# Attention with top-1 experts: row sums sent by DMA to 128 partitions of 16, inverted at once, read back 32-fold from DRAM; weights in three tiles, projections spread evenly

## The chip, the core and the metric

The kernel runs on one core of a Trainium2 chip. The time is the device time of one execution in microseconds (us); the median of several runs is compared. A profile of one further execution shows what each engine did and when.

The engines are TensorE (PE in the profile, with its weight loads as PEld), VectorE (DVE), ScalarE (ACT), GpSimd (POOL) and SyncE (SP), which here only issues transfers. Each works through its own instructions in order. TensorE writes into PSUM, of which this kernel uses eight banks of 128 x 512 numbers as one tile called `array`.

## The reference

x has 4 batches of 2,048 tokens of width 512. It is normalized, and attention and an expert layer of the normalized x are added to x:

```python
xn = _layernorm(x, axis=-1)
x = x + attn(xn, w_qkv, w_out, b_out, mask_logits) + ffn(xn, w_gate, w_expert, b_expert)

# attn: 16 heads of 32
q, k, v = split(xn @ w_qkv)                  # to heads
q, k = filter(q), filter(k)                  # rfft, times a sigmoid mask, irfft
scores = einsum('bhqd,bhkd->bhqk', q, k) / sqrt(32)
out = einsum('bhqk,bhkd->bhqd', softmax(scores), v)
return out @ w_out + b_out

# ffn: each token goes to the best of 8 experts, the first 100 tokens of each expert are
# kept; a kept row is gate * (row @ w_expert + b_expert), all other rows are 0
```

All is float32. The filter is linear, so the kernel folds it into the query and key weights at its start.

## The kernel before

**Groups, blocks, steps.** The work runs over 16 head groups k (4 batches by 4 groups of 4 heads; b, c = divmod(k, 4)), in each over 4 query blocks n of 512 queries, in each over 16 key tiles j of 128 keys. One key tile of one block is a step here (a "half" in the code: two make a window). There are 16 x 4 x 16 = 1,024 steps, 64 to a group and 16 to a block.

In each step TensorE does, for its block, two times two score products (`scores`, tiles `q` and `steps_of_keys`) into banks 0 to 3, ScalarE takes their exponentials into a tile `even` or `odd`, and the value products (`products`) of the step before follow; VectorE adds those into `num`. The scores are shifted by the maximum of their row, which has to be known before a block starts. So a second stream of products (`keys`, `q`) runs 20 steps (40 pieces, `MAX_AHEAD`) ahead; VectorE reduces each to its maximum (`max_reduce`, tile `part`), in one instruction for two banks that lie side by side, or in two (`apart`). Four steps before a block opens, the maxima are turned by TensorE (`max_close`: `square`, `neg`), split into three bfloat16 rows by POOL (`max_split`: `rest`, `row`) and sent by SP to a tile `negm`; four products of `negm` open the block (`shift`). The maxima's products, value products, projections and all the rest share banks 4 to 7 in rotation (`bank`), so a product waits until the engine that reads the bank's old content is done.

**Row sums.** The exponentials' tiles of a block are added up in pairs by a DMA that adds in place (`even<-odd`, 1 MB, issued by POOL) and then by POOL's additions (`even<-even`). Five steps after a block's end TensorE adds over the keys (`fold`, product with ones), ScalarE copies the sums to `den`. Each sum stands there on 32 partitions. VectorE inverts `den` in eight pieces of 64 columns, one per step (`invert`); POOL multiplies `num` by it (`divide`, tile `ot`) before step 14, TensorE projects with `wo` (`result`), ScalarE copies to `y`, and POOL issues a DMA that adds `y` to the output in DRAM (`add`).

**Projections.** While group k runs, the queries, keys and values of group k + 1 are made in 48 pieces of 128 tokens (`query_key`, `value`). A planner (`spread`) puts a list of steps with costs and earliest times into the agenda of the 64 steps; `costs` holds what is there already. The pieces stand in an order written out by hand (`projections`); keys can't be written before the maxima of group k are past them (`SPENT`). The weights of a group lie in one tile `wg`, reloaded once all pieces are done, so the list ends three steps before the group's end.

**A new batch.** In the third group of a batch (k = 2, 6, 10) the next batch's x is loaded tile by tile (`load_tile`), measured by VectorE, given the bias `b_out` by POOL (`bias`) and written to the output as its first sums (`first_sums`). In the fourth group x is loaded again, normalized and turned by TensorE. In group 0 the first sums of batch 0 are made in this way too.

The agenda of a step runs after its products, and `max_close` stands before it. Every engine's instructions keep the program's order (`InOrder`). In the profile nearly all of them have line 84, that helper's, so they are told apart by tile names.

Of the kernel before, what the change touches and what calls it, by code (L numbers as in the profile page):

```python
# [39 lines left out]
PART = 64  # L40
# [63 lines left out]
def attention_and_top1_experts(ctx: ExitStack, tc: tile.TileContext, a: dict, out: bass.AP):  # L104
# [90 lines left out]
    def filter_steps(c):  # L195

        held = {}

        def turned(s):
            if s == 0:  # L200
                held["wt"] = probs(c % 2 == 1)
            pt = bank()
            for r in range(NR):
                on.tensor.transpose(
                    pt[:, r * P : (r + 1) * P], raw[s, r // 2][:, r % 2, c * P : (c + 1) * P], ident
                )
            on.vector.tensor_copy(held["wt"][:, s, 0, :], pt)

        def filtered(s):
            pw = bank()  # L210
            wt = held["wt"][:, s]
            for r in range(NR):
                at = slice(r * P, (r + 1) * P)
                on.tensor.matmul(pw[:, at], lhsT=wt[:, 0, at], rhs=filt, start=True, stop=True)
            done = pw.rearrange("p (r n) -> p r n", r=NR)
            if c == 0:
                on.scalar.copy(wg[0][:, :, s, :], done)
# [12 lines left out]
    def token_stage(b):  # L230
# [20 lines left out]
        def bias(i):  # L251
            row = held[i // TQ][:, i % TQ, :]
            on.gpsimd.tensor_tensor(row, row, b_out, ALU.add)

        def first_sums(i):

            n, t = divmod(i, TQ)
            on.sync.dma_start(out=o[b, n, :, t : t + 1, :], in_=held[n][:, t : t + 1, :])
# [149 lines left out]
        return load, measure, scale, normalize, turn, route, bias, first_sums, load_tile  # L408
# [5 lines left out]
    def load_qkv_weights(k):  # L414
        wg[k] = weights.tile([P, NR, 3, P], F32, name="wg", bufs=1)
        on.sync.dma_start(out=wg[k], in_=wd[k % NG])
# [12 lines left out]
    def query_key(k, n, s, first, last):  # L429

        here, cols = slice(first * P, last * P), slice(n * QB + first * P, n * QB + last * P)
        pq = bank()[:, here]
        for r in range(NR):
            columns(pq, wg[k][:, r, s, :], xnT[:, r, cols], start=(r == 0), stop=(r == NR - 1))
# [17 lines left out]
    def value(k, n, first, last):  # L452
        if n == 0 and first == 0:
            vs[k] = qkv.tile([P, NT, P], F32, tag="v", name="v")
        pv = bank()
        for t in range(first, last):
            i = n * TQ + t
            for r in range(NR):
                columns(
                    pv[:, t * P : (t + 1) * P],  # L460
                    xnT[:, r, i * P : (i + 1) * P],
                    wg[k][:, r, 2, :],
                    start=(r == 0),
                    stop=(r == NR - 1),
                )
# [3 lines left out]
    def projections(k, tiles=1):  # L469

        if k == 0:
            order = [(query_key, 0, 1), (query_key, 0, 0)]
            order += [(query_key, n, 1) for n in range(1, NQ)] + [(query_key, 1, 0)]
            order += [(value, n) for n in range(NQ)] + [(query_key, n, 0) for n in range(2, NQ)]
        else:
            late = [(value, n) for n in range(2, NQ)] + [(query_key, 1, 0)]
            order = [(query_key, 0, 0)] + [(value, n) for n in range(2)] + (late if k not in CROWDED else [])
            order += [(query_key, n, 1) for n in range(NQ)] + (late[::-1] if k in CROWDED else [])
            order += [(query_key, n, 0) for n in range(2, NQ)]
# [72 lines left out]
    def expert_steps():  # L552


        def begin():
            w_exp = chunk("w_exp")
            on.sync.dma_start(out=w_exp, in_=a["L0_ffn_w_expert"].rearrange("(r p) n -> p r n", p=P))
            b_exp = b_out
# [130 lines left out]
    def close_steps(k, n):  # L689
# [25 lines left out]
        if (k, n) == (B * NG - 1, NQ - 2):  # L715
            steps = [(7, 1, fold)] + [(8 + i // 2, 0, invert, i) for i in range(QB // PART)]
            first = 12
# [22 lines left out]
    load, measure, scale, normalize, turn, first_route, first_bias, first_sums, load_tile = token_stage(0)  # L740
# [5 lines left out]
    wg[0] = weights.tile([P, NR, 3, P], F32, name="wg", bufs=1)  # L746
    nc.sync.dma_start(out=wg[0][:, :, 2, :], in_=w_qkv[:, :, 2 * DM : 2 * DM + P])
# [12 lines left out]
    nc.sync.dma_start(out=wd[0], in_=wg[0])  # L760
# [51 lines left out]
    for i, item in enumerate(stream[:MAX_AHEAD]):  # L812
# [6 lines left out]
        max_reduce(item, half)  # L819
# [83 lines left out]
    def keys_from(k):  # L903

        return (9 if k in CROWDED else 6) * TQ

    def plan(k):
# [4 lines left out]
        def after_keys_are_spent(steps, start):  # L912

            first = len(steps) - keys_from(k + 1)
            for i in range(NT):
                cost, _, step = steps[first + i]
                steps[first + i] = cost, start + SPENT + i // TQ * TQ, step

        if k == 0:
            for i in range(NT):  # L920
                half = 2 + i + 5 * (i // TQ)
                at(half, load_tile, i)
                at(half + 4, first_bias, i)
                at(half + 6, first_sums, i)
# [3 lines left out]
        last = start + GH - 4  # L928
        steps = []
        if k == 0:  # L930
            done = spread([(1, 0, step) for step in first_projections], 15)
            at(done[-1] + 1, load_qkv_weights, 1)
            plan_route(20, lambda i: first_route[i]())
            ready = done[-1] + 3
        if c == NG - 2 and b + 1 < B:

            at(start + 20, begin_stage, b + 1)
            for i in range(NT):
                half = start + 20 + i + 5 * (i // TQ)
                at(half, in_stage, 8, i)  # L940
                at(half + 3, in_stage, 1, i)
                at(half + 4, in_stage, 6, i)
                at(half + 6, in_stage, 7, i)
            for n in range(NQ):
                at(start + 30 + (TQ + 5) * n, in_stage, 2, n * TQ, (n + 1) * TQ)
            for i in range(2 * TQ):
                at(start + GH - 6 + i, in_stage, 8, i)
        pieces = projections(k + 1)
        if c == NG - 1:
# [3 lines left out]
            order += pieces[4:8] + [("turn", i) for i in range(12, NT)] + pieces[8:]  # L953
            steps, first = [], start + 1
            for step in order:
                if isinstance(step, tuple):
                    i = step[1]
                    steps.append((1, start + late[i] if i in late else 0, lambda i=i: in_stage(4, i)))
                else:
                    steps.append((1, 0, step))  # L960
            steps[0] = (1, first, steps[0][2])
            after_keys_are_spent(steps, start)
# [4 lines left out]
            for i in range(2 * TQ, NT):  # L967
                at(turned[i // TQ * TQ - TQ - 1] + 1 + i % TQ, in_stage, 8, i)
            plan_route(turned[NT - 1] + 2, follow_route)
        else:  # L970
            steps = [(1, ready if k == 0 else start, step) for step in pieces]
            after_keys_are_spent(steps, start)
            done = spread(steps, last)
        assert done[-4] >= start + 3 * HB and done[-8] >= start + 2 * HB
        for i in range(NT):
            here = done[len(done) - keys_from(k + 1) + i] - start - i // TQ * TQ
            assert SPENT <= here < SPENT + 3 * TQ
# [17 lines left out]
    for block in range(1, B * NG * NQ):  # L995

        costs[block * HB - 4] += 0.5
# [15 lines left out]
    for k in range(B * NG):  # L1013
        for n in range(NQ):
            num = work.tile([P, QB], F32, tag="num", name="num")
            tiles = {}
            for w in range(NW):
# [9 lines left out]
                for j in (even, odd):  # L1027
# [5 lines left out]
                    for u in range(2):  # L1033
# [7 lines left out]
                        if mate:  # L1041
                            max_reduce(mate, mh)
# [63 lines left out]
```

## Time and profile before

| | |
|---|---|
| median of 3 runs | 4,277.05 us (4,273.49 to 4,280.85) |
| profiled execution | 4,282.12 us, span 4,280.0 us, granted TensorE clock 0.993 |
| TensorE busy | 4,194.3 us, 52,270 instructions |
| VectorE busy | 3,411.0 us; of it maxima `part` 2,497.1, `num` 650.3, reciprocals 274.3 |
| POOL busy | 3,037.6 us; of it additions `even` 2,121.5 |
| ScalarE busy | 2,525.3 us |
| DMA, software queue (POOL) | 605.83 MB, 72.1% of 16 engines' span |
| DMA, hardware queue (SP) | 76.10 MB, 5.7% |

The page gives busy time, the chain of work that ended last, and groups of instructions with their mean duration. The timeline gives single instructions: start, duration, engine, operation, tile written <- tiles read, shapes, count; brackets hold the idle time before it and what ended it. A float32 product is two instructions.

### The profile page before, as it was taken

To read this page: it belongs to the slowest core of one execution; us is meant where nothing else is said; L and a number is where in the kernel's file an instruction comes from. 1 tells how busy PE (TensorE), PEld (TensorE's weight loads), DVE (VectorE), ACT (ScalarE), POOL (GpSimd) and SP (SyncE) were. 2 spreads that over 40 slices of the span, in tenths; PEclk is the share of its full clock that TensorE was granted. 3 is DMA by queue.
4 is the path that set the end of the run, shared out by engine and by line. 5 is a ranking of instruction groups with operands and counts; after the bars stand their busy time and mean duration, and the time that the engine had idled before them with its cause. 6 is when DMAs were issued, how large, how long until landed. Compare 5 with 4: busy or idle time off the path is not lost.

```text
span 4280.0 us, 120579 instructions
## 1 busy us (share of the span) xinstructions
PE 4194.3 (98%) x52270; PEld 1854.3 (43%) x52270; DVE 3411.0 (80%) x5102; ACT 2525.3 (59%) x3475; POOL 3037.6 (71%) x2110
## 2 busy tenths in 40 slices
PE   8999999999999999999999999999999999999998
PEld 4444444434444444443444444443444444444432
DVE  6767888877788888887778888887778887788885
ACT  2556655666566556557556666555755565556665
POOL 1678777876776767777677766778668776676773
PEclk9999999999999999999999999999999999999999
DMA  4767778887687778888677787888877886778788
GB/s 109 179 149 152 153 160 173 191 201 151 137 159 153 156 152 165 182 195 186 132 158 151 158 159 146 170 188 194 170 140 152 175 164 131 148 162 161 154 168 167
DMA packets 163452, 690.16 MB, mean 161 GB/s; under 512 B 27414, under 2 KB 32696, under 8 KB 97640
## 3 DMA queue, kind: packets, MB, share of 16 engines
q0 software_dynamic: 110432, 605.83, 72.1%
q1 hardware_dynamic: 51312, 76.10, 5.7%
q8 instruction: 409, 6.70, 0.6%
q14 instruction: 123, 1.01, 0.1%
q10 hardware_dynamic: 1176, 0.52, 0.1%
HBM read 59.27 MB, written 88.96 MB: 35 GB/s over the span
## 4 chain that ended last, share of the span: by engine, by line
PE 89%; DVE 6%; DMA 2%; POOL 2%; issue 1%; ACT 0%; ACTq 0%; POOLq 0%; DVEq 0%
PE array L84 89%; DVE part L84 4%; DMA even<-odd 2%; POOL even L84 1%; DVE num L84 0%; DVE stats L84 0%; DMA negm<-row 0%; DVE factor L84 0%; POOL xs L84 0%; DMA odd<-in_L_attn_w_qkv_dram 0%; DVE mv L84 0%; POOL row L84 0%; POOL rstd L84 0%; DVE even L84 0%; POOL rest L84 0%
## 5 line engine op out<-in xcount | busy, mean ns | idle before, releaser
L84 DVE TENSOR_REDUCE part<-array 128x1 f32<-128x512 f32 (+1 forms) x3336 | 2497.1, 805 | 761.6 <-PE array L84 758.3
L84 POOL TENSOR_TENSOR even<-even 128x1024 f32<-128x1024 f32 x876 | 2121.5, 2524 | 425.9 <-DMA even<-odd 417.8
L84 PE MATMUL array<-keys,q 32*128 32x512 f32 x8192 | 2089.7, 615 | 10.9 <-DVE part L84 5.5
L84 PE MATMUL array<-q,steps_of_keys 32*128 32x512 f32 x8192 | 2022.7, 618 | 3.3 <-ACT odd L84 1.7
L84 ACT ACTIVATE even<-array 128x1024 f32<-128x1024 f32 x1024 | 993.5, 1021 | 491.3 <-PE array L84 455.6
L84 ACT ACTIVATE odd<-array 128x1024 f32<-128x1024 f32 x1024 | 993.3, 1021 | 458.8 <-PE array L84 378.5
L84 PEld LDWEIGHTS array<-keys,q 32*128 32x128 f32 x8192 | 784.3, 185 | 591.3 <-DVE part L84 365.3
L84 PEld LDWEIGHTS array<-q,steps_of_keys 32*128 32x128 f32 x8192 | 707.2, 184 | 267.3 <-issue 233.1
L84 POOL DMA_DIRECT2D even<-odd x510 | 463.4, 909 | 402.2 <-ACT odd L84 321.4
L84 DVE TENSOR_TENSOR num<-num,array 128x512 f32<-128x512 f32 x960 | 650.3, 677 | 26.3 <-PE array L84 17.2
L84 PE MATMUL array<-odd,v 128*32 128x512 f32 x4096 | 549.4, 608 | 2.4 <-DVE part L84 2.4
L84 PE MATMUL array<-even,v 128*32 128x512 f32 x4096 | 547.4, 606 | 2.9 <-DVE part L84 2.9
L84 PEld LDWEIGHTS array<-xnT,wg 128*32 128x32 f32 x15808 | 439.0, 110 | 256.2 <-DVE part L84 176.2
L84 PE MATMUL array<-xnT,wg 128*32 128x128 f32 (+1 forms) x15808 | 522.0, 277 | 11.4 <-DVE part L84 10.6
L84 PEld LDWEIGHTS array<-wg,xnT 128*32 128x32 f32 x8192 | 227.9, 110 | 129.2 <-DVE part L84 94.4
L84 DVE RECIPROCAL factor<-den 128x64 f32<-128x64 f32 x504 | 274.3, 545 | 0.0
L84 PE MATMUL array<-wo,ot 128*32 128x512 f32 x2048 | 267.8, 596 | 4.0 <-POOL ot L84 4.0
L84 PE MATMUL array<-wg,xnT 128*32 128x128 f32 x8192 | 263.5, 273 | 4.4 <-DVE part L84 4.4
L84 PEld LDWEIGHTS array<-odd,v 128*32 128x32 f32 x4096 | 81.0, 108 | 394.1 <-DVE part L84 384.9
L84 PEld LDWEIGHTS array<-even,v 128*32 128x32 f32 x4096 | 80.8, 108 | 393.8 <-DVE part L84 382.7
L84 POOL DMA_DIRECT2D out_dram<-y x63 | 83.7, 1329 | 212.4 <-ACT y L84 190.9
L84 ACT COPY y<-array 128x512 f32<-128x512 f32 x252 | 147.5, 586 | 139.8 <-PE array L84 139.4
(129 smaller groups left out, 1490.5 us busy)
## 6 DMA issues: line engine op xcount, KB each, us to landing
even<-odd POOLq DMA_DIRECT2D x510, 1024.0 KB, 8.2
out_dram<-y POOLq DMA_DIRECT2D x63, 1024.0 KB, 10.1
xs<-in_L_attn_x_dram SPq DMA_DIRECT2D x112, 256.0 KB
out_dram<-xs SPq DMA_DIRECT2D x64, 256.0 KB
wg<-wd SPq DMA_DIRECT2D x15, 768.0 KB
wo<-in_L_attn_w_out_dram SPq DMA_DIRECT2D x16, 256.0 KB
negm<-row SPq DMA_DIRECT2D x192, 4.0 KB
xs<-in_L_attn_x_dram SPq DMA_DIRECT2D x2, 1024.0 KB
```

Source lines behind the costliest of these rows:

```text
L84: done = act(*args, **kwargs)
```

## The change

The eight reciprocals of a block give way to one. SP sends one copy of each row sum (`den`, every 32nd partition, 4 x 512) to 128 partitions of 16 columns (`apart`); VectorE inverts these 128 x 16 (`invert`); SP writes them to DRAM (`lay_down`) and reads them back so that each head's row of 512 lands on its 32 partitions (`to_rows`, four transfers). These steps stand one, two, three and four steps after the fold.

The weights of queries, keys and values lie in three tiles, each reloaded after its own last piece. The order of the pieces is new: values first, then queries and keys, and the list may end on the group's last step. Turns are planned at a cost of 0.5 instead of 1, the block's fixed cost at 0.25 instead of 0.5.

The first sums are x itself, copied from DRAM to DRAM 1 MB at a time; the bias is added by VectorE where the result of the first group of a batch leaves PSUM. `b_exp` has a tile of its own. Loads and statistics of a new batch stand at other steps. `max_close` follows the agenda of its step. Maxima of a step's first pair are reduced apart, those of its second pair apart only where the step has no planned cost; in the 40 pieces ahead of the first step none is kept apart on purpose.

```diff
+APART = HG * QB // P
-        def bias(i):
-            on.gpsimd.tensor_tensor(row, row, b_out, ALU.add)
-        def first_sums(i):
-            on.sync.dma_start(out=o[b, n, :, t : t + 1, :], in_=held[n][:, t : t + 1, :])
+        def first_sums(n):
+            on.sync.dma_start(out=o[b, n], in_=x[b, n])
...
-    def load_qkv_weights(k):
-        wg[k] = weights.tile([P, NR, 3, P], F32, name="wg", bufs=1)
-        on.sync.dma_start(out=wg[k], in_=wd[k % NG])
+    def load_qkv_weights(k, s):
+        wg[k, s] = weights.tile([P, NR, P], F32, name=f"w{s}", bufs=1)
+        on.sync.dma_start(out=wg[k, s], in_=wd[k % NG][:, :, s, :])
...
+            first = 2 if k in CROWDED else 3 if k % NG == 0 else 4
+            queries, vals = ([(f, n, *s) for n in range(NQ)] for f, *s in ((query_key, 0), (value,)))
+            news = [(query_key, n, 1) for n in range(NQ)]
+            if first == 4:
+                order = vals + queries[:2] + news + queries[2:]
+            else:
+                order = vals[:first] + queries[:1] + news[:3]
+                order += vals[first : first + 1] + news[3:] + vals[first + 1 :] + queries[1:]
...
-    def max_reduce(item, half):
+    def max_reduce(item, half, apart=True):
-        whole = joined(*half) if u == 0 else joined(*half, apart=True)
-        for heads, products_of in whole:
+        for heads, products_of in joined(*half, apart):
...
-        def invert(i):
-            at = slice(i * PART, (i + 1) * PART)
-            on.vector.reciprocal(held["factor"][:, at], held["den"][:, at])
+        def apart():
+            on.sync.dma_start(out=held["factor"][:, 0:APART], in_=held["den"][0::DH, :])
+        def invert():
+            at = held["factor"][:, 0:APART]
+            on.vector.reciprocal(at, at)
+        def lay_down():
+            held["all"] = scratch.tile([P, APART], F32, name="inverses")
+            on.sync.dma_start(out=held["all"], in_=held["factor"][:, 0:APART])
+        def to_rows():
+            for h in range(HG):
+                row = held["all"][DH * h : DH * (h + 1), :].rearrange("r c -> (r c)")
+                on.sync.dma_start(out=held["factor"][DH * h : DH * (h + 1), :], in_=row.partition_broadcast(DH))
...
-            on.scalar.copy(held["y"][:, t, :], project(k, held["ot"], t))
+            if k % NG == 0:
+                on.vector.tensor_tensor(held["y"][:, t, :], project(k, held["ot"], t), b_out, ALU.add)
+            else:
+                on.scalar.copy(held["y"][:, t, :], project(k, held["ot"], t))
...
-            steps = [(5, 1, fold)] + [(6 + i, 0, invert, i) for i in range(QB // PART)]
-            first = 17
+            begin, first = 5, 17
+        steps = [(begin, 1, fold)]
+        steps += [(begin + 1 + i, 0, step) for i, step in enumerate((apart, invert, lay_down, to_rows))]
...
-        last = start + GH - 4
+        last = start + GH - 1
...
-            at(done[-1] + 1, load_qkv_weights, k + 2)
+            for s in range(3):
+                at(places[s][-1] + 1, load_qkv_weights, k + 2, s)
...
-        costs[block * HB - 4] += 0.5
+        costs[block * HB - 4] += 0.25
...
-                            max_reduce(mate, mh)
+                            max_reduce(mate, mh, u == 0 or not costs[2 * window + (j == odd)])
...
+                    for step in agenda[2 * window + (j == odd)]:
+                        step()
                     if j == even and window in full:
                         splits[window + 1] = full.pop(window)
                         max_close(*splits[window + 1])
-                    for step in agenda[2 * window + (j == odd)]:
-                        step()
```

More of the change, by code (lines that the diff above doesn't have):

```diff
@@ L39 @@
 SCALE = 1.0 / math.sqrt(DH)
-PART = 64
+APART = HG * QB // P
 WIN = 2
@@ L216, in filtered @@
             if c == 0:
-                on.scalar.copy(wg[0][:, :, s, :], done)
+                on.scalar.copy(wg[0, s], done)
             else:
@@ L249, in measure @@
             on.vector.bn_aggr(mv[:, i, :], stats[:, i, :])
-        def bias(i):
-            row = held[i // TQ][:, i % TQ, :]
-            on.gpsimd.tensor_tensor(row, row, b_out, ALU.add)
-        def first_sums(i):
-            n, t = divmod(i, TQ)
-            on.sync.dma_start(out=o[b, n, :, t : t + 1, :], in_=held[n][:, t : t + 1, :])
+        def first_sums(n):
+            on.sync.dma_start(out=o[b, n], in_=x[b, n])
         def scale(first=0, last=NT, shift_on=None):
@@ L407, in token_stage @@
         route += [lambda i=i: enter(i) for i in range(NT)]
-        return load, measure, scale, normalize, turn, route, bias, first_sums, load_tile
+        return load, measure, scale, normalize, turn, route, first_sums, load_tile
     qs, vs = {}, {}
     wo = {}
-    def load_qkv_weights(k):
-        wg[k] = weights.tile([P, NR, 3, P], F32, name="wg", bufs=1)
-        on.sync.dma_start(out=wg[k], in_=wd[k % NG])
+    def load_qkv_weights(k, s):
+        wg[k, s] = weights.tile([P, NR, P], F32, name=f"w{s}", bufs=1)
+        on.sync.dma_start(out=wg[k, s], in_=wd[k % NG][:, :, s, :])
     def load_out_weights(k):
@@ L433, in query_key @@
         for r in range(NR):
-            columns(pq, wg[k][:, r, s, :], xnT[:, r, cols], start=(r == 0), stop=(r == NR - 1))
+            columns(pq, wg[k, s][:, r, :], xnT[:, r, cols], start=(r == 0), stop=(r == NR - 1))
         if s == 0:
@@ L461, in value @@
                     xnT[:, r, i * P : (i + 1) * P],
-                    wg[k][:, r, 2, :],
+                    wg[k, 2][:, r, :],
                     start=(r == 0),
@@ L467, in value, with projections @@
         on.scalar.copy(vs[k][:, n * TQ + first : n * TQ + last, :], done)
-    def projections(k, tiles=1):
+    def projections(k, tiles=1, kinds=None):
+        kinds = [] if kinds is None else kinds
         if k == 0:
@@ L475, in projections @@
         else:
[L476 to L479, printed above, removed]
+            first = 2 if k in CROWDED else 3 if k % NG == 0 else 4
[6 more added lines that the diff above has]
+                order += vals[first : first + 1] + news[3:] + vals[first + 1 :] + queries[1:]
+        kinds.extend((2 if f is value else at[1]) for f, *at in order for t in range(0, TQ, tiles))
         return [
@@ L557, in begin @@
             on.sync.dma_start(out=w_exp, in_=a["L0_ffn_w_expert"].rearrange("(r p) n -> p r n", p=P))
-            b_exp = b_out
+            b_exp = work.tile([P, DM], F32, tag="b_exp", name="b_exp", bufs=1)
             on.sync.dma_start(out=b_exp, in_=a["L0_ffn_b_expert"].partition_broadcast(P))
@@ L715, in close_steps @@
         if (k, n) == (B * NG - 1, NQ - 2):
-            steps = [(7, 1, fold)] + [(8 + i // 2, 0, invert, i) for i in range(QB // PART)]
-            first = 12
-        else:
-            steps = [(5, 1, fold)] + [(6 + i, 0, invert, i) for i in range(QB // PART)]
-            first = 17
+            begin, first = 7, 12
+        else:
+            begin, first = 5, 17
+        steps = [(begin, 1, fold)]
+        steps += [(begin + 1 + i, 0, step) for i, step in enumerate((apart, invert, lay_down, to_rows))]
         steps += [(first + t, 1, result, t) for t in range(TQ)]
@@ L737, in close_last @@
                 on.sync.dma_start(out=o[b, n, :, t - 1 : t + 1, :], in_=y[:, t - 1 : t + 1, :])
-    load, measure, scale, normalize, turn, first_route, first_bias, first_sums, load_tile = token_stage(0)
+    load, measure, scale, normalize, turn, first_route, first_sums, _ = token_stage(0)
     load(0)
@@ L745, in attention_and_top1_experts @@
     load(3, probs(False).rearrange("p u h q -> p (u h) q"))
-    wg[0] = weights.tile([P, NR, 3, P], F32, name="wg", bufs=1)
-    nc.sync.dma_start(out=wg[0][:, :, 2, :], in_=w_qkv[:, :, 2 * DM : 2 * DM + P])
+    for s in range(3):
+        wg[0, s] = weights.tile([P, NR, P], F32, name=f"w{s}", bufs=1)
+    nc.sync.dma_start(out=wg[0, 2], in_=w_qkv[:, :, 2 * DM : 2 * DM + P])
     for c in range(1, NG):
@@ L759, in attention_and_top1_experts @@
             measure(i - 2 * NG + TQ)
-    nc.sync.dma_start(out=wd[0], in_=wg[0])
+    for s in range(3):
+        nc.sync.dma_start(out=wd[0][:, :, s, :], in_=wg[0, s])
     first_projections = projections(0, TQ)
@@ L818, in attention_and_top1_experts @@
         max_matmuls(item, half)
-        max_reduce(item, half)
+        max_reduce(item, half, False)
         if i in ahead:
@@ L901, in place_experts @@
                 free += 2
-    def keys_from(k):
-        return (9 if k in CROWDED else 6) * TQ
     def plan(k):
@@ L910, in plan, with after_keys_are_spent @@
         start = k * GH
[L912 to L917, printed above, removed]
-        if k == 0:
[L920 to L924, printed above, removed]
+        def after_keys_are_spent():
+            for i, place in enumerate([j for j, s in enumerate(kinds) if s == 1]):
+                cost, _, step = steps[place]
+                steps[place] = cost, start + SPENT + i // TQ * TQ, step
+        if k == 0:
+            for n in range(NQ):
+                at(2 + (TQ + 5) * n, first_sums, n)
         if k + 1 == B * NG:
@@ L927, in plan @@
         at(start + GH // 2, load_out_weights, k + 1)
-        last = start + GH - 4
-        steps = []
+        last = start + GH - 1
+        steps, kinds = [], []
         if k == 0:
             done = spread([(1, 0, step) for step in first_projections], 15)
-            at(done[-1] + 1, load_qkv_weights, 1)
+            for s in range(3):
+                at(done[-1] + 1, load_qkv_weights, 1, s)
             plan_route(20, lambda i: first_route[i]())
@@ L938, in plan @@
             for i in range(NT):
[L939 to L945, printed above, removed]
+                half = start + 2 * HB - 2 + i + 8 * (i // (NT // 2))
+                at(half - 4, in_stage, 7, i)
+                at(half, in_stage, 1, i)
+                if i % TQ == TQ - 1:
+                    n = i // TQ
+                    at(half + 1, in_stage, 2, n * TQ, (n + 1) * TQ)
+                    at(half - 2, in_stage, 6, n)
             for i in range(2 * TQ):
-                at(start + GH - 6 + i, in_stage, 8, i)
-        pieces = projections(k + 1)
+                at(start + GH - 6 + i, in_stage, 7, i)
+        pieces = projections(k + 1, kinds=kinds)
         if c == NG - 1:
@@ L953, in plan @@
             order += pieces[4:8] + [("turn", i) for i in range(12, NT)] + pieces[8:]
+            kinds = [None] * 8 + kinds[:4] + [None] * 4 + kinds[4:8] + [None] * 4 + kinds[8:]
             steps, first = [], start + 1
@@ L957, in plan @@
                     i = step[1]
-                    steps.append((1, start + late[i] if i in late else 0, lambda i=i: in_stage(4, i)))
+                    steps.append((0.5, start + late[i] if i in late else 0, lambda i=i: in_stage(4, i)))
                 else:
                     steps.append((1, 0, step))
-            steps[0] = (1, first, steps[0][2])
-            after_keys_are_spent(steps, start)
+            steps[0] = (0.5, first, steps[0][2])
+            after_keys_are_spent()
             done = spread(steps, last)
@@ L967, in plan @@
             for i in range(2 * TQ, NT):
-                at(turned[i // TQ * TQ - TQ - 1] + 1 + i % TQ, in_stage, 8, i)
+                at(turned[i // TQ * TQ - TQ - 1] + 1 + i % TQ, in_stage, 7, i)
             plan_route(turned[NT - 1] + 2, follow_route)
@@ L971, in plan @@
             steps = [(1, ready if k == 0 else start, step) for step in pieces]
-            after_keys_are_spent(steps, start)
+            after_keys_are_spent()
             done = spread(steps, last)
         assert done[-4] >= start + 3 * HB and done[-8] >= start + 2 * HB
-        for i in range(NT):
-            here = done[len(done) - keys_from(k + 1) + i] - start - i // TQ * TQ
-            assert SPENT <= here < SPENT + 3 * TQ
+        places = [[h for h, s in zip(done, kinds) if s == kind] for kind in range(3)]
+        for i, h in enumerate(places[1]):
+            assert SPENT <= h - start - i // TQ * TQ < SPENT + 3 * TQ
+        assert places[0][3] < start + GH - MAX_AHEAD // 2 and places[0][7] < start + GH + HB - MAX_AHEAD // 2
         for n in range(NQ):
@@ L980, in plan @@
         if k + 2 < B * NG:
-            at(done[-1] + 1, load_qkv_weights, k + 2)
+            for s in range(3):
+                at(places[s][-1] + 1, load_qkv_weights, k + 2, s)
     SPENT = GH - HB - MAX_AHEAD // 2 + TQ
```

## The prediction

> **What bounds the kernel now.** I read the shares of the span and the chain that ended last, then TensorE's timeline one key tile at a time, then the waits.
>
> ```profile
> PE 4194.3 (98%) x52270; PEld 1854.3 (43%) x52270; DVE 3411.0 (80%) x5102; ACT 2525.3 (59%) x3475; POOL 3037.6 (71%) x2110
> ...
> PE 89%; DVE 6%; DMA 2%; POOL 2%; issue 1%; ACT 0%; ACTq 0%; POOLq 0%; DVEq 0%
> ```
>
> TensorE looks full, but the 98% comes from modelled ends and hides short stalls, so I measured the steps. A step is one key tile: four maximum products, four score products, four value products, and whatever the planner adds. An added projection piece is A, a result piece R, a row-sum fold F, the transposed maximum C. The first rows are a step with C and A, then two A steps; the second fence is three steps with nothing added.
>
> ```profile
> 1592.50 0.70 PE L84 MATMUL array<-keys,q 32*128 32x512 f32 x2
> ...
> 1595.32 0.38 PE L84 MATMUL array<-square,neg 128*16 128x128 f32 x2
> 1596.14 1.08 PE L84 MATMUL array<-xnT,wg 128*32 128x128 f32 x32 [0.44 <-DVE part L84]
> 1597.15 0.70 PE L84 MATMUL array<-keys,q 32*128 32x512 f32 x2
> ...
> 1600.95 0.70 PE L84 MATMUL array<-keys,q 32*128 32x512 f32 x2
> ...
> 1604.75 0.70 PE L84 MATMUL array<-keys,q 32*128 32x512 f32 x2
> ```
>
> ```profile
> 1659.55 0.70 PE L84 MATMUL array<-keys,q 32*128 32x512 f32 x2 [0.44 <-DVE part L84]
> ...
> 1662.47 0.87 PE L84 MATMUL array<-keys,q 32*128 32x512 f32 x2
> ...
> 1665.90 1.36 PE L84 MATMUL array<-keys,q 32*128 32x512 f32 x3
> ...
> 1669.49 0.73 PE L84 MATMUL array<-negm,ones_b 3*128 3x512 bf16 x4
> ```
>
> An A step takes 3.80 (1597.15 to 1600.95, then to 1604.75), and did so with a reciprocal in VectorE's stream. C and A together take 4.65 (1592.50 to 1597.15): the piece after C waits for a maximum still being reduced. Empty steps took 2.92, 3.43 and 3.59 us: TensorE needs 2.92, VectorE makes them longer.
>
> I cut all 1,024 steps this way, at the first score product. Medians: A 3.80 (330 steps), R 3.78 (181), two A 4.67 (97), C with A 4.65 (44), nothing added 3.35 (113). So a step needs 2.93 plus 0.87 for each A, R or F, about 0.30 for C, 0.11 for the shift that opens a query block; gate, rank and expert steps I fitted likewise. The 1,024 steps need 4,039 by these prices and took 4,161. The 122 over are all that the change can win between the first step (at 100.4) and the end:
>
> - 57 steps with C: 26
> - 71 empty steps: 37
> - the ends of the three groups that load a next batch: 33
> - three steps from 233 to 253, with a wait of 1.46 for nothing shown ("issue") and a slowed clock: 6
> - the last head group: 10
> - all other steps: 10
>
> The third item is POOL's. It waits for a DMA pair sum, comes late to the split of the maxima, and TensorE waits for the DMA that carries them:
>
> ```profile
> 869.45 4.67 POOL L84 TENSOR_TENSOR even<-even 128x1024 f32<-128x1024 f32 x2 [5.36 <-DMA even<-odd]
> ...
> 889.36 0.42 POOL L84 TENSOR_TENSOR rest<-rest,row 16x128 f32<-16x128 f32 x1
> ...
> 890.68 0.28 POOL L84 CAST row<-rest 16x128 bf16<-16x128 f32 x1
> ```
>
> ```profile
> 892.66 0.61 PE L84 MATMUL array<-negm,ones_b 3*128 3x512 bf16 x4 [6.49 <-DMA negm<-row]
> ```
>
> ```profile
> 886.00:893.00 7.00, 0.51 (x8) 0.35 (x8) 1.01 (x2) 0.64 (x1) 6.79 (x9) 0.86 0.56 107
> 893.00:900.00 7.00, 7.00 (x44) 2.10 (x36) 3.86 (x6) 2.55 (x3) 6.56 (x4) 0.66 1.05 248
> ```
>
> The granted clock (third number from the right) falls to 0.66 after the gap. The step that opens there took 5.16 against 3.04, so each such gap costs about 9, not 6.5.
>
> **The change, part by part.** TensorE's instructions are the same in number and kind, so the 4,039 stays.
>
> *Reciprocals.* 504 of 0.545 us go from VectorE (274 us). 63 of 128x16 come; the trace has one of that size (total) at 0.25, so 16 us. Most of this is off the path: the eight steps of each block that held one are mostly A steps, at 3.80 already. It is on the path in empty steps of the last group, where nothing else fills: I take 4 of its 10.
>
> *The round trip.* Six SP transfers per block. VectorE's reciprocal now waits for the first (128 runs of 64 bytes), and behind it stand the next step's maximum reductions, for whose banks TensorE waits. The time allowed is what the trace shows between the copied sums and the second old reciprocal, which has the new one's slot:
>
> ```profile
> 1568.98 0.58 ACT L84 COPY den<-array 128x512 f32<-128x512 f32 x1 [0.67 <-PE array L84]
> ```
>
> ```profile
> 1576.79 0.55 DVE L84 RECIPROCAL factor<-den 128x64 f32<-128x64 f32 x1
> ```
>
> That is 7.2 us (over 63 blocks: median 7.17, 90% between 6.7 and 8.0). Nearest transfer: negm<-row, also with four partitions on one side. In the trace's packet records its last packet starts 1.27 after issue with the software queue idle; in the 61 cases with it busy 2.86 in the median, 5.7 at nine in ten, 6.7 at most. At this place the queue is busy, since a pair sum is issued at 1568.63. The Trainium skill (DMA: Bandwidth & Descriptors, "Queues, rings and completion order" and "Why a DMA increments its semaphore by 16 and not by 1") speaks against the change: an engine switches between queues only after a packet of some 9 to 17 descriptors, and four source partitions give four engines, here 32 descriptors each, so two to four turns. A software packet of 8 KB takes 0.65 in the records, eight per engine and pair sum 5.2; by the rule two full turns would be over 10, late everywhere by 3. By the row it is 3 to 5, with one or two for 32 runs in place of four, in time in most blocks. I follow the row, since its 16 runs lay within 0.2 us in most busy cases, and charge 4 us (about one block in ten, under 1 us); bounds 0 and 63 x 3 = 190. Less than nothing is excluded: it only adds a wait. The other hops have from then to the division, six steps or 22 us, for two transfers; by the 2 us fixed cost that the page fits to the software path ("Anatomy of one DMA") or the worst row of 6.7, they fit. SP's weight loads and negm transfers stand behind these waits but have a block and some 16 us; the share of the DMA engines grows by about 1% (12 MB more beside the 76 MB that cost 5.7%). Were that cover gone, POOL's product would be late, and the maxima after it.
>
> *Even projections, three weight tiles.* The weight tiles let pieces run to the last step. In the built order empty steps outside the last group fall from 80 to 33 (counting nine in the stage ends), A steps rise from 330 to 408, double A fall from 97 to 75. An isolated empty step should cost what such a one costs now, 0.45 over: 15 instead of 37, gain 22 (bounds 15 and 28; the separate reductions in it add 0.06 to VectorE, by 2.48 for four against 2.42).
>
> *C behind the step's piece.* The C step no longer holds a piece waiting 0.44 behind it: C stands where that reduction has ended, and the next step wants a num bank about 0.2 later. 57 steps at 26 become 14: gain 12 (bounds 5 and 22).
>
> *x to out from DRAM, the bias in the result.* POOL loses 64 additions of 1.546, the b_out rows (92.5 us), most of them in the three batch-loading groups where it runs late by 6 to 10. The copies and tile loads also come earlier than the group's end. I take the stage ends from 33 to 3: gain 30 (bounds 5 and 33). VectorE adds the bias in 64 R steps, ACT saves as many copies. 0.68 beside reductions of 2.4 and num at 0.6 makes 3.7 in a step of 3.78, so no rate is lost; but the bank is freed about 0.3 later, once per block: 16 blocks, cost 5 (bounds 0 and 16).
>
> *Statistics* now fall one tile per step, 0.84 of VectorE in 16 A or R steps per batch: 3.1 + 0.8 against 3.8. Cost about 3 in all. *Four A in one step* happen four times instead of once; the one of today lies where TensorE waited on "issue". Cost 3 (bounds 0 and 18). *Head:* joined reductions in the 40 leading pairs save 0.06 each, at most 2; taken as nothing.
>
> Sum: 4 + 22 + 12 + 30 - 4 - 5 - 3 - 3 = 53, plus 7 of the "other steps", which held reciprocals beside statistics: 60. The profiled execution took 4,282 (span 4,280.0 and 2.1 around it), 5 over the median of 4,277. It would become 4,222, the median 4,217.
>
> **The rivals.**
>
> 1. *The stage ends stay.* A whole 1 MB copy from DRAM to DRAM goes through the same queues and delays pair sums as the 256 KB writes did. For: DMA share 0.92 just before that gap. Against: POOL is what was late, and it loses the work. 30 less: 4,247. Chance 0.17.
> 2. *Slower: the sums land late.* Place: VectorE's reciprocal two steps after the fold. Price: 63 times the lateness beyond 7.2 plus the 0.7 that VectorE has spare in an A step. The 60 are eaten at 60/63 = 0.95 beyond that, a landing at 8.9 on average; at the rule's 10 or more, and a granted clock that falls after such gaps, about 4,330. For: the rule, and a busy queue at that moment. Against: the worst of 192 small transfers was 6.7. Chance 0.08.
> 3. *More is won.* C and empty steps go to what TensorE needs: 4,190. Chance 0.20.
> 4. *The headline does nothing.* Reciprocals weren't on the path, and placement brings little because new bank conflicts replace the old: C and empty steps keep two thirds, stage ends half: 4,255 or, with a few "issue" waits, 4,270. Chance 0.10.
>
> My own case, near 4,217: 0.45.
>
> **How the numbers follow.** The likeliest is 4,217. The range reaches from case 3 (4,186) to most of cases 1 and 4 (4,258); what lies outside is case 2 and the tails, under 0.2. A measurement of this kernel can tell about 0.2%, 8.6 us, from no change. Slower: case 2 with a bit less than its whole, 0.07. Same: parts of 2 and 4, 0.04. Faster: 0.89.
>
> **What would show it.** Right: C steps near 4.3, a single empty step per head group, no negm wait of 5 us or more at the three stage ends, VectorE near 3,190 busy (3,411 - 258 + 43), POOL near 2,945, and VectorE's new reciprocal not waiting for its transfer. Wrong: "DVE factor <- DMA factor<-den" among the large waits, TensorE waiting for part in A steps, a half-speed clock at new places, or stage ends as long as now.

## The result, and the profile after

Before, the median of four runs was 4,277.45 us (4,273.49 to 4,280.85); after, it is 4,406.02 us (4,396.58 to 4,408.13). The ratio is 1.0297, with a 95% interval of 1.0279 to 1.0314: the changed kernel is 3% slower. The profiled execution took 4,396.58 (span 4,394.8), the lowest of the four. The prediction named 4,217; its second rival, the sums that land late, is what happened.

First the page of the kernel after: busy time of each engine, then the chain that ended last.

```profile
PE 4206.9 (96%) x52270; PEld 1876.0 (43%) x52270; DVE 3233.8 (74%) x4758; ACT 2491.3 (57%) x3411; POOL 2965.7 (67%) x2046
...
q1 hardware_dynamic: 100764, 89.47, 7.0%
...
PE 81%; DMA 14%; DVE 3%; issue 2%; ACT 1%; POOL 0%; SPq 0%; DVEq 0%; ACTq 0%; POOLq 0%
```

VectorE and POOL were relieved, though by less than forecast (3,190 and 2,945 were named), and the time went up. The chain says where to look: TensorE's share fell from 89% to 81% and that of transfers rose from 2% to 14%. The waits of the same kernel (us in total, times, longest) name the transfer:

```profile
PE array L84 <- DVE part L84: 152.6, 71, 6.4
...
DVE factor L84 <- DMA factor<-den: 145.1, 37, 11.5
...
DVE factor L84 <- issue: 62.5, 21, 7.1
...
POOL ot L84 <- DMA factor<-inverses: 16.0, 1, 16.0
...
PE array L84 <- POOL ot L84: 13.3, 2, 11.6
...
DVE factor L84 <- DMA xs<-in_L_attn_x_dram: 3.0, 1, 3.0
```

VectorE stood before its new reciprocal in 59 of 63 blocks, 210.6 us in all. In 21 of them the view has no name for what ended the wait ("issue"), in one it names a load of x. TensorE waited 152.6 for maxima, against 29.7 before. The two totals are one event seen from two engines, as one block shows, on ScalarE, SP, POOL, VectorE and TensorE in this order:

```profile
1602.03 0.59 ACT L84 COPY den<-array 128x512 f32<-128x512 f32 x1 [0.67 <-PE array L84]
```

```profile
1602.68 0.57 SPq L84 DMA_DIRECT2D factor<-den  x1
```

```profile
1599.13 1.30 POOL L84 DMA_DIRECT2D out_dram<-y  x1 [4.16 <-ACT y L84]
1601.68 0.87 POOL L84 DMA_DIRECT2D even<-odd  x1 [1.25 <-ACT odd L84]
```

```profile
1609.19 0.68 DVE L84 TENSOR_TENSOR num<-num,array 128x512 f32<-128x512 f32 x1
1613.05 0.25 DVE L84 RECIPROCAL factor<-factor 128x16 f32<-128x16 f32 x1 [3.19 <-DMA factor<-den]
1613.22 2.42 DVE L84 TENSOR_REDUCE part<-array 128x1 f32<-128x512 f32 x4
```

```profile
1610.89 0.59 PE L84 MATMUL array<-keys,q 32*128 32x512 f32 x2
1613.90 1.07 PE L84 MATMUL array<-odd,v 128*32 128x512 f32 x8 [2.42 <-DVE part L84]
```

The sums are copied by 1602.62 and SP issues at once. The reciprocal needs 0.25 but starts 10.4 after the issue. The four reductions behind it are late by the 3.19 that VectorE stood still, and TensorE, whose value products need one of their banks, loses 2.42. Nothing else is late in this step. In 58 blocks TensorE waits for a maximum at this place, 144.1 us in all.

The trace's packet records say why 128 runs of 64 bytes take so long. (A run is one stretch of bytes that lie side by side; a transfer has landed when its last run is through.) In this block the first run starts 4.90 after the issue. Then runs go four by four: 4.90 to 5.34, 5.51 to 5.95, 6.13 to 6.57, 6.74 to 7.18, and so on, a turn every 0.61, for 28 runs. Packets of 8 KB, which are the pair sum's, take 0.63 each in the same stretch. From 9.19 on the other 100 runs go through in 0.63. So, as I read the records, the runs alternate one by one with the pair sum's packets until that is done. The spacing fits four engines with one run to a turn, though the records do not name the engine. Over the 63 blocks the first run starts 4.8 after issue in the median, the last at 10.0 (one in ten later than 12.7), and the reciprocal at 10.5.

Not all went against the forecast. A step with C and A, in TensorE's timeline of after (C in the second row; the others are the first products of this step and of the next two):

```profile
1562.58 0.70 PE L84 MATMUL array<-q,steps_of_keys 32*128 32x512 f32 x2
...
1566.26 0.38 PE L84 MATMUL array<-square,neg 128*16 128x128 f32 x2
...
1566.81 0.70 PE L84 MATMUL array<-q,steps_of_keys 32*128 32x512 f32 x2
...
1570.60 0.70 PE L84 MATMUL array<-q,steps_of_keys 32*128 32x512 f32 x2
```

It took 4.23, then an A step 3.79. Before, the step with C took 4.65.

I cut all kernels below into steps in the way the prediction does, with the same prices. The table gives the time over what TensorE needs, in us of each kernel's profiled execution. "Steps 7 to 9" are those around the new reciprocal; the rows do not overlap. The prices are those fitted to before, so a small negative number means no more than zero. The profiled execution of after was the lowest of its four, so its column lies 9 us below the median time.

| | before | after | e1 | e2 | e3 | e4 | e5 | e6 | e7 | e8 |
|---|---|---|---|---|---|---|---|---|---|---|
| steps 7 to 9 of a block | 6.1 | 170.5 | 2.8 | 4.8 | 218.9 | 29.7 | 2.9 | 6.1 | 6.1 | 18.1 |
| last head group | 10.2 | 24.1 | 18.6 | 6.2 | 22.6 | 6.5 | 10.2 | 10.8 | 10.5 | -2.4 |
| three stage ends | 33.3 | 2.8 | 16.0 | 22.1 | 6.7 | 13.3 | 16.8 | 31.8 | 18.2 | 2.8 |
| C elsewhere | 26.1 | 11.6 | 11.2 | 11.1 | 24.7 | 10.5 | 11.3 | 11.3 | 27.1 | 10.4 |
| empty elsewhere | 34.6 | 7.2 | 7.2 | 8.3 | 32.9 | 7.2 | 7.6 | 33.5 | 34.5 | 7.2 |
| R elsewhere | 1.7 | 10.3 | 12.7 | 12.6 | 2.0 | 11.5 | 12.3 | 0.0 | 5.2 | 10.4 |
| other | 10.2 | 11.3 | 19.8 | 17.5 | 6.2 | 16.7 | 17.0 | 15.1 | 13.3 | 13.8 |
| sum | 122 | 238 | 88 | 83 | 314 | 95 | 78 | 109 | 115 | 60 |

### The profile page after: what moved, and what is told of

It is laid out like the page before. It is cut to its first block, busy times and chain, and to the rows that moved or that the text cites. A ratio compares the mean times of both kernels' runs of the same rounds, so it can differ in the third digit from the quotient of the medians.

```text
span 4394.8 us, 120708 instructions
## 1 busy us (share of the span) xinstructions
PE 4206.9 (96%) x52270; PEld 1876.0 (43%) x52270; DVE 3233.8 (74%) x4758; ACT 2491.3 (57%) x3411; POOL 2965.7 (67%) x2046
## 4 chain that ended last, share of the span: by engine, by line
PE 81%; DMA 14%; DVE 3%; issue 2%; ACT 1%; POOL 0%; SPq 0%; DVEq 0%; ACTq 0%; POOLq 0%
PE array L84 81%; DMA factor<-den 13%; DVE part L84 2%; ACT den L84 1%; DVE factor L84 0%; DVE stats L84 0%; DMA xs<-in_L_attn_x_dram 0%; DMA odd<-in_L_attn_w_qkv_dram 0%; POOL rstd L84 0%; DMA mask<-_L_attn_mask_logits_dram 0%; DVE xs L84 0%; DVE mv L84 0%; POOL ot L84 0%; SPq L84 0%; DVE num L84 0%
## 5 line engine op out<-in xcount | busy, mean ns | idle before, releaser
L84 PE MATMUL array<-q,steps_of_keys 32*128 32x512 f32 x8192 | 2043.5, 620 | 2.1 <-issue 2.0
L84 POOL DMA_DIRECT2D even<-odd x510 | 449.3, 881 | 723.3 <-ACT odd L84 603.9
L84 PE MATMUL array<-odd,v 128*32 128x512 f32 x4096 | 560.3, 619 | 144.1 <-DVE part L84 144.1
L84 DVE TENSOR_TENSOR num<-num,array 128x512 f32<-128x512 f32 x960 | 650.7, 678 | 34.5 <-PE array L84 31.0
L84 PEld LDWEIGHTS array<-xnT,w 128*32 128x32 f32 x15808 | 453.2, 111 | 268.3 <-DVE part L84 167.3
L84 PE MATMUL array<-xnT,w 128*32 128x128 f32 (+1 forms) x15808 | 534.0, 281 | 0.8 <-ACT xnT L84 0.7
L84 PEld LDWEIGHTS array<-w,xnT 128*32 128x32 f32 x8192 | 233.1, 111 | 148.7 <-DVE part L84 104.2
L84 PE MATMUL array<-wo,ot 128*32 128x512 f32 x2048 | 267.5, 595 | 13.3 <-POOL ot L84 13.3
L84 PE MATMUL array<-w,xnT 128*32 128x128 f32 x8192 | 271.8, 275 | 1.5 <-DVE num L84 1.2
L84 ACT COPY q<-array 128x128 f32<-128x128 f32 (+1 forms) x250 | 67.2, 269 | 243.7 <-PE array L84 243.7
L84 ACT COPY keys<-array 128x128 f32<-128x128 f32 (+1 forms) x244 | 66.3, 272 | 216.8 <-PE array L84 215.0
```

The costliest lines, as they stand in the source:

```text
L84: done = act(*args, **kwargs)
```

## The experiments

The theory after the result: the transfer of the sums lands at 10 where 7.9 is free, because it shares its engines with the pair sum, and that alone turns a gain into a loss. Rivals: the loss lies in the new placement or in the bank order, or the round trip's later hops cost it, or the added traffic on the hardware queue does.

**e1: the same transfers, the reciprocal two steps later.**

```diff
+        late = 0 if begin == 7 else 2
         steps = [(begin, 1, fold)]
-        steps += [(begin + 1 + i, 0, step) for i, step in enumerate((apart, invert, lay_down, to_rows))]
+        steps += [(begin + 1, 0, apart)]
+        steps += [(begin + 2 + late + i, 0, step) for i, step in enumerate((invert, lay_down, to_rows))]
```

> The changed kernel with the one reciprocal, the write to DRAM and the read back two steps later; the first transfer and the division stay. Theory 'late landing': the sums land 10.5 us (median) after their issue where VectorE wants them at 7.2, and all of the loss is that wait; two steps give 7.6 more, so the excess of about 165 in the eighth steps goes and the time is 4,220 to 4,240. Rival 'something else of the change': the wait only shows there, so it moves to the tenth step and the time stays over 4,350.

Measured: 4,245.63, ratio to before 0.9915 (0.9896 to 0.9934), 6 above the expected range. The waits of e1:

```profile
PE array L84 <- DMA negm<-row: 25.7, 7, 7.4
...
POOL ot L84 <- DMA factor<-inverses: 21.9, 5, 16.2
...
DVE factor L84 <- DMA factor<-den: 12.2, 2, 11.6
...
DVE factor L84 <- issue: 1.2, 1, 1.2
```

The transfer itself is no quicker: first run at 4.91, last at 10.02. The reciprocal, now 15.6 after the issue, no longer waits but in three cases, and 160 us are gone. So the traffic costs nothing that shows; the lateness does. What stays is the last head group (18.6), where one block has no later step to give: POOL waits 16.2 for the inverses, TensorE 11.8 for POOL.

**e2: the change with the eight old reciprocals in place of the round trip.**

```diff
-        steps += [(begin + 1 + i, 0, step) for i, step in enumerate((apart, invert, lay_down, to_rows))]
+        pace = 2 if begin == 7 else 1
+        steps += [(begin + 1 + i // pace, 0, invert, i) for i in range(QB // PART)]
```

> The changed kernel with the eight reciprocals of 128x64 of the kernel before in place of the round trip; all else stays. Late landing: 4,215 to 4,240, since the other parts gave what was predicted of them and the eight reciprocals lie in steps with a piece. Something else of the change: over 4,350. If the round trip, once in time, is worth something itself, this is up to 10 over the kernel with the reciprocal two steps later.

Measured: 4,238.87, ratio 0.9898 (0.9882 to 0.9915). VectorE works 220 us more than in after (3,453.4 against 3,233.8), and the kernel is 4% faster than it (0.9898 against 1.0297). The rest of the change is worth about 44 us (before, run beside it, had 4,282.97).

**e3: before with the round trip alone.**

```diff
-        def invert(i):
-            at = slice(i * PART, (i + 1) * PART)
-            on.vector.reciprocal(held["factor"][:, at], held["den"][:, at])
+        def apart():
...
+        def invert():
...
+        def lay_down():
...
+        def to_rows():
...
```

> The kernel before with the round trip alone. Late landing: 63 times about 2.7, so 4,420 to 4,460, with the excess in the eighth steps. Something else of the change: 4,260 to 4,300.

Measured: 4,476.48, ratio 1.0458 (1.0440 to 1.0477), a little above what was expected. Its chain and waits:

```profile
PE 79%; DMA 13%; DVE 5%; issue 3%; ACT 1%; POOL 0%; SPq 0%; DVEq 0%; ACTq 0%; POOLq 0%
```

```profile
DVE factor L84 <- DMA factor<-den: 127.0, 34, 11.6
...
DVE factor L84 <- issue: 83.8, 25, 5.3
```

The loss is the round trip's, whatever stands around it. Its last run came at 9.98, as in after, and yet steps 7 to 9 cost 48 more than there. The traces take this apart. In these steps TensorE waited 146 us for VectorE, against 131 in after. The rest is clock: the granted clock fell to 0.5 in these steps of 37 of the 59 blocks outside the last group, which lost 69 us beyond their waits; in after it fell in 19, which lost 35. Why the waits are longer here stays open.

**e4: 16 partitions of 128 in place of 128 of 16,** so 16 runs of 512 bytes.

```diff
-APART = HG * QB // P
+APART = 128
+ROWS = HG * QB // APART
...
-            on.sync.dma_start(out=held["factor"][:, 0:APART], in_=held["den"][0::DH, :])
+            on.sync.dma_start(out=held["factor"][0:ROWS, 0:APART], in_=held["den"][0::DH, :])
```

> The changed kernel with the sums spread over 16 partitions of 128 instead of 128 of 16, so 16 runs of 512 bytes instead of 128 of 64; the reciprocal grows to about 0.9. If each run waits for one packet of the pair sum (0.61 per run and engine), four runs an engine end near 4.8 + 3 x 0.61 = 6.6 after issue and VectorE waits little: 4,220 to 4,250. If the number of runs does not matter, only when the queue comes free: over 4,330.

Measured: 4,257.27, ratio 0.9948 (0.9928 to 0.9967), 7 above the expected range. The first run starts as late as before (4.84 after issue). The last starts at 7.2 instead of 10.0, since four turns of four runs, 0.65 apart, are all there are. The wait shrinks by four fifths, to 40.4:

```profile
DVE factor L85 <- DMA factor<-den: 31.3, 27, 2.9
...
DVE factor L85 <- issue: 9.1, 11, 1.6
```

So few runs are through before the pair sum ends, where 128 have to wait for its end. The reciprocal of 16x128 takes 0.94 where that of 128x16 takes 0.25; how much of the 29.7 in steps 7 to 9 is this and how much the wait that is left, this run does not say.

**e5: e1, with the old reciprocals for the blocks that close in the last head group.**

```diff
+        if (k, n) >= (B * NG - 2, NQ - 1):
+            pace = 2 if begin == 7 else 1
+            steps += [(begin + 1 + i // pace, 0, direct, i) for i in range(QB // PART)]
+        else:
+            steps += [(begin + 1, 0, apart)]
+            steps += [(begin + 4 + i, 0, step) for i, step in enumerate((invert, lay_down, to_rows))]
```

> The changed kernel with the reciprocal two steps later, and in the last head group, whose steps are shorter, the eight old reciprocals in place of the round trip. The last group's steps cost 6 over what TensorE needs instead of 19 with the round trip, so 12 less than the 4,245 of the kernel with the later reciprocal: 4,228 to 4,238, the fastest so far. If the last group is held up by something else than its round trips: 4,240 to 4,250.

Measured: 4,239.26, ratio 0.9901 (0.9886 to 0.9916), between the two ranges expected; e2 had 0.9898. The last group costs 10.2 over its need, less than e1's 18.6 but not the 6 expected. With every sum in time, and about 200 us less of VectorE work than e2, the round trip is worth nothing that can be measured.

**e6: before with `max_close` behind the agenda, alone.**

```diff
+                    for step in agenda[2 * window + (j == odd)]:
+                        step()
                     if j == even and window in full:
                         splits[window + 1] = full.pop(window)
                         max_close(*splits[window + 1])
-                    for step in agenda[2 * window + (j == odd)]:
-                        step()
```

> The kernel before with the turn of the maxima behind the step's other work, alone. As predicted of this part: 44 steps with a piece and the turn lose most of 0.55 each, so 12 to 20 less than before (ratio near 0.996). If the wait only moves to the next step's products: no difference.

Measured: 4,266.76, ratio 0.9962 (0.9948 to 0.9975), 14.5 below the 4,281.31 of before, run beside it. In the table the C steps fall from 26.1 to 11.3, so this term stands.

**e7: before with the DRAM copy of x and the bias on VectorE, alone** (`b_exp` in its own tile with it; the steps of loads and statistics stay).

```diff
-        def bias(i):
-            row = held[i // TQ][:, i % TQ, :]
-            on.gpsimd.tensor_tensor(row, row, b_out, ALU.add)
...
-            on.sync.dma_start(out=o[b, n, :, t : t + 1, :], in_=held[n][:, t : t + 1, :])
+            on.sync.dma_start(out=o[b, n], in_=x[b, n])
```

> The kernel before with the first sums copied from x in DRAM and the bias added where the result leaves PSUM, alone; tile loads and statistics stay at their steps. If POOL's bias additions made the stage ends late, as the prediction said: 33 fall to 3, so 25 to 30 less (ratio near 0.9935). If it is the queue of pair sums, which the copies use as well: the stage ends keep 15 to 25, so 5 to 15 less.

Measured: 4,275.22, ratio 0.9986 (0.9977 to 0.9995), 6 below before, as expected if pair sums are the cause. The stage ends fall only from 33.3 to 18.2, and of that 3.5 are given back in the R steps. The waits of e7, and POOL at the place that the prediction showed for before:

```profile
POOL even L84 <- DMA even<-odd: 457.6, 196, 7.2
...
PE array L84 <- DMA negm<-row: 15.2, 5, 5.5
```

```profile
883.12 4.67 POOL L84 TENSOR_TENSOR even<-even 128x1024 f32<-128x1024 f32 x2 [2.90 <-DMA even<-odd]
887.76 0.42 POOL L84 TENSOR_TENSOR rest<-rest,row 16x128 f32<-16x128 f32 x1
...
889.09 0.28 POOL L84 CAST row<-rest 16x128 bf16<-16x128 f32 x1
```

```profile
891.06 0.62 PE L84 MATMUL array<-negm,ones_b 3*128 3x512 bf16 x4 [3.84 <-DMA negm<-row]
```

POOL lost its bias additions, and its waits for pair sums grew from 434.7 to 457.6. It still reaches the split late, and TensorE still waits 3.84 here, where it waited 6.49.

**e8: after, with the pair sum before the transfer left out.**

```diff
-                    pair(*pairs.pop(window))
+                    both = pairs.pop(window)
+                    if window % NW != 3:
+                        pair(*both)
```

> The changed kernel, leaving out in each block the one pair sum (of seven or eight) that is issued just before the row sums are sent, so those exponentials are missing from the row sums. If it is this transfer that the 64-byte runs wait for: they land within 3 us, the excess in the eighth steps goes, 4,215 to 4,250. If it is SP's own queue or the four engines that hold them: landing stays near 10 and the time over 4,380.

Measured: 4,220.05, ratio 0.9854 (0.9839 to 0.9869); the time is read for the mechanism only. The wait in question:

```profile
DVE factor L84 <- DMA factor<-den: 18.3, 8, 5.1
```

With that pair sum away, the first run starts at 4.00 and the last at 4.94, in the median, in place of 4.8 and 10.0. That is later than the 3 expected, and another transfer explains it: in this stretch the records are full of 2 KB packets of the software queue (430 of them after the issue, in the median), which are the addition of `y` to the output, issued 3.6 before the sums' transfer in the block above. In three blocks of both kernels (the first, second and 52nd) `y` was sent over 7 us before or not at all, so the traces hold all four cases. The last run starts, in us after the issue:

| | no pair sum just before (e8) | pair sum just before (after) |
|---|---|---|
| `y` not just before: three blocks | 1.5 | 6.0, 6.3, 6.7 |
| `y` just before: the others, median | 5.0 | 10.0 |

(Left out are the 63rd block, whose steps are shorter, and one of e8 in which `y` follows the sums.) So it takes both transfers to bring the landing to 10: `y` adds some 3.5, the pair sum some 5. Three blocks are few, but the same blocks of e1 and e3 land at 6.0 to 6.7 too. One more thing falls out: with one pair sum in eight gone, the stage ends cost 2.8, which fits a lateness of POOL that hangs on the pair sums.

## Why the prediction was wrong

*The round trip: the failed step.* The prediction found the right place, the right wait and nearly the right price for lateness, and then chose the wrong landing. It had two to choose from, the row of negm<-row (3 to 5) and the skill's rule (over 10, "late everywhere by 3"), and wrote: "I follow the row, since its 16 runs lay within 0.2 us in most busy cases, and charge 4 us". The landing was 10.0, the cost 172: 4,406.0 against 4,233.8, which is e2's 0.9898 times 4,277.45. The row was the wrong neighbour in two ways. It has 16 runs where this transfer has 128, and a turn here took 0.61 for four runs. And e8 shows that the delay comes from what is in the queue at that very moment, the addition of `y` and the pair sum; the median over all negm cases with the queue busy did not ask for a pair sum issued one microsecond before. The trace of before showed that issue, and the prediction cited it. It showed one more, which the prediction does not name, the addition of `y` (POOL, before; the sums were copied by 1569.56):

```profile
1566.08 1.29 POOL L84 DMA_DIRECT2D out_dram<-y  x1 [5.04 <-ACT y L84]
1568.63 0.87 POOL L84 DMA_DIRECT2D even<-odd  x1 [1.26 <-ACT odd L84]
```

Even 16 runs would have landed at 7.2 here (e4), against the 3 to 5 assumed.

*The rule.* The Trainium skill (DMA: Bandwidth & Descriptors, "Queues, rings and completion order") gave the right sign by the wrong count: the prediction took from it two to four turns of 9 to 17 descriptors each. The records here read as single runs between single packets of 8 KB, which would be up to 32 turns, and the count only mattered until the pair sum ended. That end, not the number of turns, set the landing in the median block.

*The price of lateness.* Rival 2 priced 63 times the lateness beyond 7.9. With the median reciprocal at 10.5 this is 63 x 2.6 = 164; counted block by block, the 59 blocks outside the last group were late by 171. Steps 7 to 9 rose by 164. That the two agree so well is in part luck: TensorE waited 131 there, and in 19 of these blocks, where the granted clock fell to 0.5, the steps lost another 35. The rival names such a clock but gives it no term, and in e3, with a lateness of 166, the same steps rose by 213. Its total of about 4,330 was low: it set a cost of 113 against a gain of 60, though its own price at a landing of 10 gives 63 x 2.1 = 132, and the runs show 172 against 44. It also reckoned with a landing at 10 rather than a reciprocal at 10.5, and left out the last head group (+14), where one block has no later step to give. Its chance, 0.08, rested on "the worst of 192 small transfers was 6.7", the same wrong neighbour. The range ended at 4,258 though the text had given the round trip a bound of 190.

*Stage ends, x to out from DRAM: 30 forecast, 11 to 17 found* in e2 and e5, about 15 in e7. This is the prediction's first rival, in its size at least. In after the term reads 30.5, just as forecast, but not for the reason forecast: e3, which keeps POOL's bias additions, shows 26.6 as well. TensorE's stalls give POOL time to catch up, it seems, so only the kernels without the stall show the term.

*Even projections: 22 forecast.* Empty steps outside the ends fall from 34.6 to 8.3 in e2, 26 of gain; right. *C: 12 forecast,* 15 by the table in e2 and 14.5 measured in e6; right, in the 4.3 us that it named for such a step (4.23).

*Bias, statistics, and the four-A steps: 5, 3 and 3 forecast, against 7 won from other steps.* R steps cost 11 more in e2, of which the bias alone makes 3.5 (e7); other steps 7 more instead of 7 less. The new placement gives back about 15 here. The placement was not run by itself, so this is a count in the table, not a cause shown.

*Reciprocals: 4 forecast.* The last group gains 4 in e2 too, which still has all the old ones, so that gain is not theirs. In the other groups their absence is worth nothing that can be measured: e2 and e5 differ by 0.4 us in the median.

Without the round trip the forecast terms made 60 and the runs made 44. The sign, though, was lost in a single step, the landing.

Two versions beat both kernels by about 1%: e2, which keeps all of the change but its headline, and e5, which keeps the headline too, in time. e2 is the simpler and has the same time.

## What to carry to other kernels

When a transfer replaces work on an engine that isn't the bound, there is nothing to win and a landing time to lose; ask first what the freed engine was holding up. Price the landing by everything that is in the queues at the moment of issue and by the number of separate runs, not by the median of a transfer with fewer of them, and place the instruction that waits for it behind that time: two steps of delay were worth 160 us here (after to e1), because the next user stood 22 us away. A waiting instruction on an in-order engine costs what stands behind it, so look at the neighbour in the stream rather than at the instruction.

## What was not expected of the hardware

One pair sum of 1 MB held up a transfer of 8 KB by five microseconds. In the stretch both share, runs of 64 bytes go four every 0.61, about the length of a packet of 8 KB (0.63), and once the sum was done 100 runs went in 0.63. Runs of 512 bytes took their turns in nearly the same rhythm (0.65), so here the number of runs mattered more than their size. Without the pair sum, 128 runs took about 1.

A long gap also costs clock. In windows of 7 us over the largest stall of after (columns: window, length, busy time of PE, PEld, VectorE, ScalarE and POOL with counts, granted clock, DMA share, GB/s):

```profile
2933.70:2940.70 7.00, 1.97 (x20) 0.69 (x16) 0.35 (x1) 2.21 (x3) 4.77 (x6) 1.00 1.11 220
2940.70:2947.70 7.00, 5.65 (x52) 2.85 (x56) 3.21 (x5) 0.27 (x1) 4.67 (x2) 0.52 0.67 137
2947.70:2954.70 7.00, 7.00 (x127) 3.59 (x124) 6.03 (x8) 4.44 (x6) 3.92 (x3) 0.99 0.85 240
```

The window after the gap runs at 0.52, then it is over. The length of a wait alone does not tell which ones cost clock: in steps 7 to 9 of after and e3, blocks with 2.0 to 6.4 us of waits saw the clock fall, and others with up to 3.6 did not. Over the whole span the granted clock was 0.993 before, 0.985 after and 0.978 in e3.
